# Four fused convolution layers on one core: late jobs forced by their own kind, and an earlier due step for the next chunk's first gates

## The chip, the cores and the metric

The kernel runs on one core of a Trainium2 chip. The metric is the device time of one execution in microseconds (us), the median of several runs. Everything is computed in float32.

## The reference, cut to what matters

The input is x with shape (8, 384, 32, 32): eight images of 384 channels and 1024 positions. Each of four layers adds its result to x, after a group norm over 32 groups.

```python
# layer 0: mamba block (layer 2 is the same with a layer norm ahead and an MLP behind)
xin, z = split(xseq @ in_proj_w.T)              # 384 -> 2 x 768
u   = silu(causal_conv3(xin) + conv_b)
dbc = u @ x_proj_w.T                            # dt (24), B (16), C (16)
dt  = softplus(dt @ dt_proj_w.T + dt_proj_b)
h   = exp(dt * A) * h + dt * u * B              # along 1024 positions, 768 x 16 states
y   = (sum_n h * C + u * D) * silu(z)
x   = x + y @ out_proj_w.T
# layer 1: 1x1 conv, filter on 8x8 patches, 3x3 depthwise conv, gated GELU, 1x1 conv
# layer 2: layer norm, mamba block, then gelu(t @ mlp_w1.T) @ mlp_w2.T
# layer 3: 3x3 depthwise conv
```

## The kernel before

**Chunks and steps.** The two mamba layers set the frame. Each image is cut into two chunks of 512 positions, c = 0 and 1, which gives 16 chunks for layer 0 (n = 0 to 15) and 16 for layer 2 (n = 16 to 31). Each chunk has 24 steps (`NQ`), one for each group of 32 of the 768 inner channels, so there are 768 steps. A step t does the following:

- `times(t + 1)` (L619): two multiplications on POOL (L623) of dt*u by B for the next step.
- `scan(t)` (L637): four scans along 512 positions on DVE (L643), two multiplications by C on DVE (L654) and one of twice the width on POOL (L660).
- `gather(t - 1)` (L664): TensorE sums over the 16 states into y.
- `begin(t + 3)` (L610): a DMA on SP's queue loads dt*u, spread over the states, from the scratch tensor `dud` into a tile g.
- `decay(t + 1)` (L627): TensorE spreads dt into four PSUM banks dA, and ACT takes the exponential.

The four banks dA exist once, so decay(t + 1) waits for the scans of step t.[...]

**Jobs.** All other work is cut into jobs, Python generators whose pieces are put between the parts of a step: `measure` (group statistics of a later image), `front` (L487: load, norm, first projection, convolution, SiLU, dt, B and C of the next chunk), `gates` (L440: z and its SiLU, in two halves of 12 steps each), `finish` (L722: the output projection and, in layer 2, the MLP), `layer1` and `layer3` (once for each image). A job has a first step, a due step ("last") and a kind. The class `Jobs` keeps them: `step` (L133) gives pieces away in order of their due steps, as long as the measured need of such a piece fits the room of the step, counted as TensorE and VectorE time (`ROOM`, L68, and `begin`, L124). The need of a piece is what the same piece took in the last finished job of the same kind (L102). A piece may answer "wait", and the next job in order is asked. `until` (L148) ignores the room: it runs pieces in order of due steps until a condition holds.

**Where work is forced.** At steps 4 and 16 of a chunk `until` asks for the gates of the half in use (L1027). At every step it asks for the `dud` of the step three later (L1041); at steps 21 to 23 that is the next chunk's front. The due steps are given in the main loop, counted from the chunk's first step t: gates of the second half t + 8; the next chunk's front t + 14; the next chunk's first gates t + 26 (`t + NQ + 2`); `measure` t + 28; the end of the chunk before 10, 16 or 23 steps after it; `layer1` and `layer3` of an image near the end of the chunk two later (L732 to L736).

**What jobs wait for.** `front` starts when the second gates of the chunk before are done (L490), and its first projection waits until the chunk two before has finished its output projection ("free", L504, L720). `out_proj` waits for the end of the chunk before and for one of three tiles x (L687), which `layer1` or `layer3` releases when it ends (L858, L991). The first gates wait for the norm and for half of the chunk before (L442). Three PSUM banks are shared by all jobs.

All jobs' matmuls are recorded at one line, L177; all activations at L241; most of the jobs' VectorE work at L85. They are told apart by their tiles: `ps_z` gates, `ps_in`, `ps_x`, `ps_bc`, `ps_dt` front, `ps_out` output projection, `ps_up` and `ps_dn` MLP, `ps_t`, `ps_o` layer 1, `ps_dw` the convolution of layer 1 (with `tp`) or layer 3 (with `xp`).

Of the kernel before, what the change touches and what calls it, by code (L numbers as in the profile page):

```python
# [40 lines left out]
NSUB = 4  # L41
NQ = ND * NSUB
QUADS = [(k, s) for k in range(ND) for s in range(NSUB)]
NH = ND // 2
# [9 lines left out]
def _flat(ap):  # L54
    return ap.rearrange("p a b -> p (a b)")
# [8 lines left out]
WAIT = "wait"  # L64
# [25 lines left out]
class Jobs:  # L90
# [54 lines left out]
                    if went:  # L145
                        break

    def until(self, done):  # L148

        while not done():  # L150
            if not any(self.piece(job) for job in self.in_order()):
                raise RuntimeError("no job goes on")


# [1 line left out]
def tile_conv_preact_d4(ctx: ExitStack, tc: tile.TileContext, a: dict, out: bass.AP):  # L156
# [12 lines left out]
    jobs = Jobs(work)  # L169
# [9 lines left out]
    def ps_tile(name):  # L179

        while live["ps"] >= NBANK:
            yield WAIT
        live["ps"] += 1
        return psg.tile([P, 512], F32, tag="ps", name=name)
# [4 lines left out]
    def pipe(units, deep=2):  # L189


        flying = []
        units = deque(units)
        while units or flying:
            went = bool(flying)
            for f in list(flying):
                if f["stages"]:
                    f["stages"].popleft()(f["ps"])
                settle(f)
                if not f["stages"]:  # L200
                    flying.remove(f)
            if units and live["ps"] < NBANK and len(flying) < deep:
                went = True
                name, stages = units.popleft()
                live["ps"] += 1
                ps = psg.tile([P, 512], F32, tag="ps", name=name)
                stages[0](ps)
                f = {"stages": deque(stages[1:]), "ps": ps, "bank": True}
                settle(f)
                if f["stages"]:  # L210
                    flying.append(f)
            if units or flying:
                yield None if went else WAIT
# [8 lines left out]
    def both(*stages):  # L222


        def run(ps):
            for stage in stages:
                stage(ps)

        return run
# [3 lines left out]
    def act(out_, in_, func, **kw):  # L233

        if func in (AF.Exp, AF.Ln):
            if act_set["now"] != "exp":
                nc.scalar.preload_act_table_set(SET_EXP)
                act_set["now"] = "exp"
        elif func not in (AF.Identity, AF.Copy, AF.Square, AF.Abs):
            act_set["now"] = func  # L240
        nc.scalar.activation(out_, in_, func, **kw)  # L241

    def exp_again():

        nc.scalar.preload_act_table_set(SET_EXP)
        act_set["now"] = "exp"
# [152 lines left out]
    def measure(s):  # L399

        blocks = [(h, k) for h in range(2) for k in range(KC)]
        loaded = {}

        def load(q):
            if q < len(blocks):
                h, k = blocks[q]
                x = loaded[h, k] = wk.tile([P, T], F32, tag="spm", name="xk", bufs=2)
                nc.sync.dma_start(
                    x, s["src"][s["b"], k * P : (k + 1) * P, h * T : (h + 1) * T]
                )  # L410

        live["spm"] = True
        load(0)
        load(1)
        yield NEXT

        def block(h, k):
            return loaded.pop((h, k)), lambda: load(blocks.index((h, k)) + 2)

        def all_read():  # L420
            live["spm"] = False

        s["stats"] = yield from group_stats(block, all_read, NEXT)

    def project(s, d, at):


        def run(ps):
            for k in range(KC):
                mm(  # L430
                    ps,
                    s["w"]["in"][:, k, at + d * P : at + (d + 1) * P],
                    s["xn"][:, k, :],
                    start=k == 0,
                    stop=k == KC - 1,
                )

        return run

    def gates(s, h):  # L440

        while "normed" not in s or (  # L442
            h == 0 and s["n"] > 0 and "half" not in chunks[s["n"] - 1]
        ):
            yield WAIT
        z = s["z", h] = wk.tile([P, NH, T], F32, tag="z", name="z", bufs=2)

        def evict(d):
            return lambda ps: act(z[:, d, :], ps, AF.Copy)

        yield from pipe(
            ("ps_z", [both(project(s, h * NH + d, DI), evict(d))]) for d in range(NH)
        )
        yield EARLY
        act(_flat(z), _flat(z), AF.Silu)
        exp_again()
        s["gates", h] = True
        yield
# [28 lines left out]
    def front(s):  # L487

        c, n = s["c"], s["n"]
        while n > 0 and ("gates", 1) not in chunks[n - 1]:  # L490
            yield WAIT
        xn = s["xn"] = load_half(s)
        if n % (B * NCH) == 0:
# [53 lines left out]
            act(_flat(uh[h]), _flat(uh[h]), AF.Silu)  # L547
        exp_again()
        yield NEXT
        ps = yield from ps_tile("ps_x")  # L550
        for d in range(ND):
            mm(ps[:RX, :], w["x"][:, d, :], u[d], start=d == 0, stop=d == ND - 1)
# [52 lines left out]
        while flying:  # L605
            flying = [f for f in flying if next(f, f) is not f]
            yield NEXT


    def begin(s, i):  # L610
        k, sub = QUADS[i]
        t = s["g", i] = wk.tile([P, 4, T], F32, tag="g", name="g", bufs=AHEAD + 1)
        nc.sync.dma_start(
            _flat(t),
            s["dud"][k][E8 * sub : E8 * (sub + 1)].rearrange("e j t -> e (j t)")
            .unsqueeze(0).to_broadcast([NS, E8, 4 * T]),
        )

    def times(s, i):  # L619

        for j in (0, 2):
            g = s["g", i][:, j : j + 2, :]
            nc.gpsimd.tensor_mul(  # L623
                g, g, s["bc"][:, 0, :].unsqueeze(1).to_broadcast([P, 2, T])
            )
# [11 lines left out]
    def scan(s, i):  # L637

        g = s["g", i]
        own = SHARE[s["pre"]][s["c"]][i % NSUB]  # L640
        for j in range(4):
            q = 4 * i + j
            nc.vector.tensor_tensor_scan(  # L643
                dAs[j] if j < own else g[:, j, :],
                dAs[j],
                g[:, j, :],
                0.0 if s["c"] == 0 else carry[:, q : q + 1],
                ALU.mult,
                ALU.add,
            )  # L650
            if j < own:
                if s["c"] < NCH - 1:
                    nc.vector.tensor_copy(carry[:, q : q + 1], dAs[j][:, T - 1 : T])
                nc.vector.tensor_mul(g[:, j, :], dAs[j], s["bc"][:, 1, :])  # L654
        if s["c"] < NCH - 1:
            nc.vector.tensor_copy(  # L656
                carry[:, 4 * i + own : 4 * i + 4].unsqueeze(2), g[:, own:4, T - 1 : T]
            )
        g = g[:, own:4, :]
        nc.gpsimd.tensor_mul(  # L660
            g, g, s["bc"][:, 1, :].unsqueeze(1).to_broadcast([P, 4 - own, T])
        )
# [307 lines left out]
    def layer3(s):  # L970
# [24 lines left out]
    chunks = [  # L995
        {"pre": pre, "src": src, "b": b, "c": c, "n": (q * B + b) * NCH + c}
        for q, (pre, src) in enumerate((("l0_", a["x"]), ("l2_", x_mid)))
        for b in range(B)
        for c in range(NCH)
    ]  # L1000
# [14 lines left out]
    for t in range(total):  # L1015
        s, i = steps[t]
        n = s["n"]
        later = chunks[n + 1] if n + 1 < len(chunks) else None
        if i == 0:
            jobs.add("gates", gates(s, 1), t + 1, t + 8)  # L1020
            if s["c"] == 0 and n + NCH < len(chunks):
                jobs.add("measure", measure(chunks[n + NCH]), t, t + NQ + 4)
            if later:
                jobs.add("front%d" % (later["pre"] == "l2_"), front(later), t + 3, t + 14)
                jobs.add("gates", gates(later, 0), t + 13, t + NQ + 2)
        if i % (NH * NSUB) == NSUB:
            jobs.until(lambda: ("gates", i // (NH * NSUB)) in s)  # L1027
        if t + 1 < total:
            times(*steps[t + 1])
        scan(s, i)  # L1030
        jobs.begin(ROOM["turn" if n == B * NCH else s["pre"]])
        jobs.step(t, 2.0)
        if t > 0:
            p, q = steps[t - 1]
            gather(p, q)
            if q == NQ - 1:
                end = 10 if p["pre"] == "l0_" else 23 if p["c"] == 0 else 16
                jobs.add("end%d" % (p["pre"] == "l2_"), finish(p), t + 1, t + end)
        if t + AHEAD < total:
            p, q = steps[t + AHEAD]  # L1040
            jobs.until(lambda: p.get("dud", {}).get(QUADS[q][0]))  # L1041
            begin(p, q)
        jobs.step(t)
        if t + 1 < total:
            decay(*steps[t + 1])
# [133 lines left out]
```

## Time and profile before

| | us |
|---|---|
| median of 3 runs | 7789.29 |
| lowest, highest run | 7782.02, 7790.03 |
| the profiled execution | 7774.96 |
| its span, first to last instruction | 7773.2 |
| PE busy in it | 7244.1 |
| DVE busy | 5787.0 |
| POOL busy | 5638.8 |
| ACT busy | 4034.0 |
| mean granted TensorE clock, share of full | 0.922 |

The span is of the profiled execution, which is 14 us faster than the median. A matmul's end in the profile is modelled and matmuls are pipelined, so PE's busy time includes waiting. Busy times are of engines that work beside each other and don't add up. In lines of the timeline the columns are start in us, duration in us, engine, line, operation, tile written and tiles read, shape and count; what stands in square brackets is idle time of the engine before it and what ended it. A float32 matmul counts as two instructions (1152 of them for the 576 matmuls of the output projection).

### The profile page before, as it was taken

The numbers are of one execution on the slowest core, as the hardware profiler recorded it, in microseconds if no ns is written. First come the engines' busy times: TensorE is split into PE (matmuls) and PEld (weight loads), VectorE is DVE, ScalarE is ACT, GpSimd is POOL, SyncE is SP. The second block draws the span as 40 slices with busy tenths as digits, with TensorE's granted clock in tenths as the row PEclk, the third lists the DMA queues.
The fourth block names the chain that finished last, engine by engine and source line by source line (L and its number), as shares of the span: only waits on it lengthen the run. The fifth ranks groups of instructions, "written<-read, shape, count | busy, mean of one in ns | idle before, by whom it ended". The sixth has DMA issues, their size and how long they took to land. (4 is left out here: it accounts for less than half of the span.)

```text
span 7773.2 us, 76689 instructions
## 1 busy us (share of the span) xinstructions
PE 7244.1 (93%) x25762; PEld 3001.0 (39%) x25762; DVE 5787.0 (74%) x7350; ACT 4034.0 (52%) x6980; POOL 5638.8 (73%) x2710
## 2 busy tenths in 40 slices
PE   7989999999999999999999989999999999999998
PEld 2223333333333333333334434444444444444445
DVE  5988788888777878778746765767777677776871
ACT  4445555554554555455545544555555555555543
POOL 5888878788787878778646764767767677676770
PEclk8888889999888999988899999999999999999999
DMA  5666556556565646556536654666656666565662
GB/s 141 141 151 144 138 134 142 136 135 150 127 146 127 141 120 148 128 139 146 129 78 167 174 135 120 165 156 172 165 150 174 155 170 164 149 164 146 171 168 67
DMA packets 288919, 1122.50 MB, mean 144 GB/s; under 512 B 37386, under 2 KB 90970, under 8 KB 190220
## 3 DMA queue, kind: packets, MB, share of 16 engines
q1 hardware_dynamic: 288524, 1117.59, 58.4%
q8 instruction: 204, 3.34, 0.2%
q14 instruction: 191, 1.56, 0.1%
HBM read 1041.96 MB, written 75.50 MB: 144 GB/s over the span
## 5 line engine op out<-in xcount | busy, mean ns | idle before, releaser
L623 POOL TENSOR_TENSOR g<-g,bc 128x1024 f32<-128x1024 f32 x1536 | 3586.8, 2358 | 197.2 <-DMA g<-dud 181.2
L660 POOL TENSOR_TENSOR g<-g,bc 128x1024 f32<-128x1024 f32 x768 | 1806.2, 2352 | 1441.1 <-DVE carry L656 806.6
L241 ACT ACTIVATE dA<-dA,w_A 128x512 f32<-128x512 f32 x3072 | 1860.7, 662 | 1543.3 <-PE dA L177 1530.1
L177 PE MATMUL dA<-dt,selr 32*128 32x512 f32 x6144 | 1573.3, 677 | 70.6 <-DVE g L654 61.9
L643 DVE TENSOR_TENSOR_SCAN dA<-dA,carry,g 128x512 f32<-128x512 f32 x768 | 986.6, 1285 | 616.0 <-issue 275.6
L643 DVE TENSOR_TENSOR_SCAN dA<-dA,g 128x512 f32<-128x512 f32 x768 | 940.6, 1225 | 477.5 <-issue 167.7
L654 DVE TENSOR_TENSOR g<-dA,bc 128x512 f32<-128x512 f32 x1536 | 1053.9, 686 | 29.8 <-DVE dA L643 0.5
L177 PE MATMUL y<-g,sely 128*32 128x512 f32 x6144 | 934.1, 637 | 43.0 <-POOL g L660 37.5
L643 DVE TENSOR_TENSOR_SCAN g<-dA,carry,g 128x512 f32<-128x512 f32 x768 | 940.6, 1267 | 0.0
L643 DVE TENSOR_TENSOR_SCAN g<-dA,g 128x512 f32<-128x512 f32 x768 | 893.3, 1204 | 0.0
L177 PEld LDWEIGHTS dA<-dt,selr 32*128 32x128 f32 x6144 | 470.2, 191 | 984.4 <-DVE g L643 517.3
L177 PE MATMUL ps_dn<-h,mw 128*128 128x256 f32 x2304 | 573.9, 401 | 75.3 <-DMA mw<-in_l_mlp_w 58.6
L177 PE MATMUL ps_up<-t,mw 128*128 128x256 f32 x2304 | 566.8, 394 | 59.0 <-DMA mw<-in_l_mlp_w 44.2
L177 PE MATMUL ps_z<-xf,w_in 128*128 128x512 f32 x1152 | 586.1, 649 | 27.3 <-DVE dt L85 23.6
L177 PE MATMUL ps_in<-xf,w_in 128*128 128x512 f32 x1152 | 566.9, 633 | 27.3 <-DVE u L85 25.5
L177 PE MATMUL ps_dw<-tp,diag 96*96 96x512 f32 x1152 | 572.8, 638 | 15.2 <-ACT diag L241 15.2
L177 PE MATMUL ps_out<-u,w_out 128*128 128x512 f32 x1152 | 543.7, 619 | 10.2 <-DVE x L85 10.2
L177 PEld LDWEIGHTS ps_dn<-h,mw 128*128 128x128 f32 x2304 | 439.5, 197 | 277.0 <-issue 118.8
L177 PEld LDWEIGHTS ps_up<-t,mw 128*128 128x128 f32 x2304 | 425.8, 192 | 268.4 <-issue 148.9
L177 PE MATMUL ps_dw<-xp,diag 128*128 128x512 f32 x864 | 407.5, 622 | 42.2 <-ACT diag L241 40.9
L241 ACT ACTIVATE u<-ps_in,w_vec 128x512 f32<-128x512 f32 x192 | 149.4, 778 | 484.2 <-PE ps_in L177 484.2
L177 PEld LDWEIGHTS y<-g,sely 128*32 128x32 f32 x6144 | 134.2, 111 | 648.5 <-issue 461.1
(99 smaller groups left out, 6463.1 us busy)
## 6 DMA issues: line engine op xcount, KB each, us to landing
g<-dud SPq DMA_DIRECT2D x768, 1024.0 KB, 7.1
mw<-in_l_mlp_w SPq DMA_DIRECT2D x384, 384.0 KB, 7.4
dud<-du SPq DMA_DIRECT2D x768, 64.0 KB, 1.7
xk<-in_x SPq DMA_DIRECT2D x48, 256.0 KB, 4.2
xf<-in_x SPq DMA_DIRECT2D x16, 768.0 KB, 8.4
x<-in_x SPq DMA_DIRECT2D x16, 768.0 KB, 8.5
x_mid<-x SPq DMA_DIRECT2D x16, 768.0 KB, 4.6
xk<-x_mid SPq DMA_DIRECT2D x48, 256.0 KB, 5.0
```

The source lines that it names most:

```text
L177: nc.tensor.matmul(out_, lhsT, rhs, start=start, stop=stop)
L241: nc.scalar.activation(out_, in_, func, **kw)
L623: nc.gpsimd.tensor_mul(g, g, s["bc"][:, 0, :].unsqueeze(1).to_broadcast([P, 2, T]))
L643: nc.vector.tensor_tensor_scan(dAs[j] if j < own else g[:, j, :], dAs[j], g[:, j, :], 0.0 if s["c"] == 0 else carry[:, q : q + 1], ALU.mul ...
L654: nc.vector.tensor_mul(g[:, j, :], dAs[j], s["bc"][:, 1, :])
L660: nc.gpsimd.tensor_mul(g, g, s["bc"][:, 1, :].unsqueeze(1).to_broadcast([P, 4 - own, T]))
```

## The change

The change touches the planner and two waits in `front`; no arithmetic is added or removed.

- `until` takes a kind. Jobs of that kind are asked first, then all jobs in order of due steps.
- The kind "gates" is split into "gates0" and "gates1", so that each half has a history of needs of its own. Forcing at steps 4 and 16 names the half, forcing of `dud` names the front.
- The next chunk's first gates are due at t + 20 (`t + NQ - 4`) instead of t + 26. They now stand ahead of jobs due at t + 21 to t + 25.
- `front` also waits for the image's statistics before it starts, and ahead of `ps_x` for the end of the front of the chunk before ("spread"). Both are waits of the planner: no instruction is added, the piece is placed later.

```diff
-    def until(self, done):
+    def until(self, done, kind=None):
 
         while not done():
-            if not any(self.piece(job) for job in self.in_order()):
+            late = [job for job in self.in_order() if job["kind"] == kind]
+            if not any(self.piece(job) for job in late + self.in_order()):
                 raise RuntimeError("no job goes on")
...
         c, n = s["c"], s["n"]
-        while n > 0 and ("gates", 1) not in chunks[n - 1]:
+        while n > 0 and ("gates", 1) not in chunks[n - 1] or "stats" not in chunks[n - c]:
             yield WAIT
...
         exp_again()
         yield NEXT
+        while n > 0 and "spread" not in chunks[n - 1]:
+            yield WAIT
         ps = yield from ps_tile("ps_x")
...
             flying = [f for f in flying if next(f, f) is not f]
             yield NEXT
+        s["spread"] = True
...
         if i == 0:
-            jobs.add("gates", gates(s, 1), t + 1, t + 8)
+            jobs.add("gates1", gates(s, 1), t + 1, t + 8)
...
-                jobs.add("gates", gates(later, 0), t + 13, t + NQ + 2)
+                jobs.add("gates0", gates(later, 0), t + 13, t + NQ - 4)
         if i % (NH * NSUB) == NSUB:
-            jobs.until(lambda: ("gates", i // (NH * NSUB)) in s)
+            h = i // (NH * NSUB)
+            jobs.until(lambda: ("gates", h) in s, "gates%d" % h)
...
             p, q = steps[t + AHEAD]
-            jobs.until(lambda: p.get("dud", {}).get(QUADS[q][0]))
+            jobs.until(
+                lambda: p.get("dud", {}).get(QUADS[q][0]), "front%d" % (p["pre"] == "l2_")
+            )
             begin(p, q)
```

## The prediction

> **What bounds the kernel now.** I read the page first (shares, slices, the groups of POOL), then the timeline around the two kinds of place where work is forced, then the stretches table for the same places.
>
> ```profile
> span 7773.2 us, 76689 instructions
> ...
> PE 7244.1 (93%) x25762; PEld 3001.0 (39%) x25762; DVE 5787.0 (74%) x7350; ACT 4034.0 (52%) x6980; POOL 5638.8 (73%) x2710
> ...
> PEclk8888889999888999988899999999999999999999
> ...
> L623 POOL TENSOR_TENSOR g<-g,bc 128x1024 f32<-128x1024 f32 x1536 | 3586.8, 2358 | 197.2 <-DMA g<-dud 181.2
> L660 POOL TENSOR_TENSOR g<-g,bc 128x1024 f32<-128x1024 f32 x768 | 1806.2, 2352 | 1441.1 <-DVE carry L656 806.6
> ```
>
> The span has 768 steps, 10.1 us each. POOL needs 2 x 2.358 + 2.352 = 7.07 us in every step; I round to a floor of 7.1. PE's 93% hides waiting, so I take its need from spacing in the timeline:
>
> ```profile
> 3731.86 1.06 PE L177 MATMUL y<-g,sely 128*32 128x512 f32 x8
> 3732.86 1.14 PE L177 MATMUL dA<-dt,selr 32*128 32x512 f32 x8
> 3733.93 2.84 PE L177 MATMUL ps_out<-u,w_out 128*128 128x512 f32 x6
> ...
> 3737.70 15.72 PE L177 MATMUL ps_in<-xf,w_in 128*128 128x512 f32 x36
> ```
>
> The scan's own matmuls take 3733.93 - 3731.86 = 2.07 us a step. Other work goes at about 0.43 us an instruction (15.72/36), and a 128x512 matmul is two of them: 0.86 us. I call that a unit. A step with u units then needs max(7.1, 2.07 + 0.86u); they balance at 5.85 units. The instruction order gives u for every step (between two groups of dA matmuls). A step's time is from the first exponential of one dA group to that of the next. Chunk 23 (5420.6 to 5652.2 us) has 161 units and no large burst: 231.6 us against a need of 24 x 2.07 + 161 x 0.86 = 188.2, so an ordinary step carries 43.4/24 = 1.81 us of waiting between engines. All units sum to 4785.6 in both kernels: the work is the same, so only the waiting and steps below the floor can change the time.
>
> Two places matter. "22.4" is chunk 22, step 4. There the old order forces 36 units (30 of layer 3's convolution and 6 of gates):
>
> ```profile
> 5200.54 10.57 PE L177 MATMUL ps_dw<-xp,diag 128*128 128x512 f32 x24
> ...
> 5212.31 15.72 PE L177 MATMUL ps_dw<-xp,diag 128*128 128x512 f32 x36 [1.20 <-ACT diag L241]
> 5227.86 5.31 PE L177 MATMUL ps_z<-xf,w_in 128*128 128x512 f32 x12
> ...
> 5235.20 2.37 POOL L660 TENSOR_TENSOR g<-g,bc 128x1024 f32<-128x1024 f32 x1 [28.46 <-DVE carry L656]
> ```
>
> POOL idles 28.46 us, but PE waits only 1.20 us. At 16.21 a late front is forced, 31 units:
>
> ```profile
> 3757.08 5.36 PE L177 MATMUL ps_x<-u,w_x 128*57 128x512 f32 x12 [3.66 <-ACT u L241]
> 3763.21 0.69 PE L177 MATMUL ps_bc<-dbc,w_dt 32*128 32x512 f32 x1 [0.77 <-ACT dbc L241]
> 3768.44 1.28 POOL L583 TENSOR_TENSOR du<-dt,u 128x512 f32<-128x512 f32 x1 [13.14 <-DVE dt L85]
> ```
> ```profile
> 3734.00:3769.30 35.30, 30.86 (x86) 11.26 (x86) 17.18 (x25) 17.71 (x23) 10.06 (x10) 0.95 0.23 63
> 3769.30:3774.30 5.00, 3.02 (x11) 0.71 (x4) 4.76 (x8) 2.46 (x6) 5.00 (x3) 0.50 0.22 54
> 3774.30:3788.10 13.80, 13.80 (x37) 4.99 (x38) 12.90 (x22) 5.58 (x9) 9.91 (x6) 0.70 0.70 154
> ```
>
> (Columns: length, then busy PE, PEld, DVE, ACT, POOL; granted clock; DMA share; GB/s.) The front is a chain, and PE waits inside it; the planner then gives step 22 no units at all, and PE's granted clock falls to 0.50 and 0.70.
>
> **What the skill says.** The Trainium skill, "Perfetto Trace Analysis", Identifying the Most-Contended Engine: matmul busy time is no measure of closeness to the peak. It agrees: the need is 4785.6 x 0.86 + 768 x 2.07 = 5705 us, the page shows 7244.1 busy. "TensorE: Matmul & The Clock Gate", Part 1, What's actually happening: the clock is gated by recent activity and halves after an idle window. It agrees: 0.50 in the 5.00 us after the front, 0.97 to 0.99 in full chunks. Same page, Part 2, Step-by-step: matmuls keep program order. It agrees: at 22.4 the y matmuls stand behind all 72 forced instructions, until 5233.10.
>
> **The change part by part.** It adds and removes no matmul.
>
> Forcing by kind at step 4 and 16: the bursts at 20.4 (64.5 units) and at 22.4, 24.4, 26.4, 28.4, 30.4 (36 each) are gone; only gates are forced. Price: steps 4 to 6 of those five chunks take 55.3, 53.6, 53.6, 53.6, 55.3 us for 48 units, a need of 3 x 2.07 + 41.3 = 47.5; 6.8 us of waiting on average, against 3 x 1.81 = 5.4. Gain 1.4 x 5 = 7. At 20.4 to 20.6 it is 87.8 us for 77.5 units, need 72.9: 14.9 of waiting, gain 9. Together -15 (sum of the unrounded terms -16).
>
> The earlier end of the first gates (20 steps instead of 26) and the new order leave the front of the next chunk late. In the new order, step 21 forces a front in every chunk from 19 to 30: 13, 19, 13, 38.5, 16, then 44.5 and 16 in turn. These were ordinary steps of 6 to 8.5 units in chunks 20 to 30, so 11 front bursts are new. Each is followed by a step of 0 or 1 and one of 7 units. Price: steps 21 to 23 of chunk 16 take 54.1 us for 38 units, need 38.9: 15.2 of waiting. The smaller ones in chunks 6, 8, 10 (31.1, 34.9, 42.8 us for 16.5, 18.5, 17 units) give 10.7, 12.8, 22.0, mean 15.2 again. The same three steps without a burst, in chunks 21 to 24 (31.7, 29.4, 31.9, 29.5 us for 21 to 21.5 units), give 7.5, 4.7, 7.7, 4.8, mean 6.2. So 9.0 each, bounds 4.5 and 15.8: 11 x 9.0 = +99. This contains the spills and loads: g<-dud stands on SP's queue behind dud<-du and the MLP weights, POOL waited 1.65 us for it after 16.21.
>
> Steps below the floor: in chunks 19 to 30 outside step 22, the old order has 2 steps of 3 units, the new one 18. A step of 3 units loses 7.1 - 2.07 - 2.58 = 2.45 us of PE that no later step gives back: 16 x 2.45 = +39. Bounds 0 (the neighbour's PE work slides in) and 64 (12.12 and 12.13, 3 and 6 units, took 7.4 + 11.6 us, 4 over two ordinary ones).
>
> Layer 0 and 1: bursts at 8.21 and 10.21 grow from 13 to 25 units. Their waiting goes from 12.8 and 22.0 to the 24.4 of 12.21 (55.6 us for 29 units): +14, bounds 0 and 20. At 16.21 it grows from 31 to 43 with the same chain: 0.
>
> The end: after the last scan 217.5 units stand alone instead of 171, because 46.5 units of layer 3 and the MLP are no longer forced earlier. Those units cost the same 0.86 us at 20.4, uncovered as well, so only waits count: one more wait of down on GELU (3.72 us before ps_dn in the end of the old trace) and the seams of the convolution (1.20 us): +6, bounds 0 and 12.
>
> New waits: "stats" and "spread" are waits of the planner and add no instruction; what they hold back stands in the order and is counted above.
>
> Sum: 99 + 39 + 14 + 6 - 15 = +143 us. The profiled execution is 7774.96 us (span 7773.2): 7918. The median shown, 7789.29, is 14 above it: 7932, which I round to 7930.
>
> **The rivals.** *Faster: slack.* One mechanism, in the ordinary steps of chunks 20 to 30: bursts take units away, 6.7 per step become about 6.45, and PE then absorbs what DVE, ACT and POOL are late. Price: some 11 x 21 = 231 steps, so it decides from 143/231 = 0.62 us a step. For it: 12.1 to 12.20 take 8.34 us for 5.85 units, 1.24 us of waiting. Against: chunk 18 has 6.56 units and 2.18 us of waiting. If waiting falls from 1.81 to 1.0, -0.81 x 231 = -187 + 143 = -44: 7745.
>
> *No change.* The front bursts cost only their low bound and the low steps nothing: 11 x 4.5 - 15 + 0 to 6 = +35 to +41; with slack of 0.15 us a step, about 0: 7789. For it: PE is busy 30.86 of 35.30 us at 16.21. Against: the 4.9 us at 16.22 with hardly any units.
>
> *Slower still: the clock.* PE's holes keep the clock down. Chunk 19, with bursts and low steps, was granted 0.93 and took 256.2 us for 158 units; chunk 23, at 0.99, 231.6 for 161. If all eleven chunks become like it, 11 x 24.6 = +271 in place of 99 + 39: +276, 8065.
>
> That the change doesn't do what it says can be excluded for step 4: the order shows it. That it moves the lateness instead of removing it is my forecast.
>
> **How the numbers follow.** Forecast 0.63, slack 0.15, no change 0.10, clock 0.12. The forecast's own range adds the bounds without all extremes at once: +35 to +250, 7824 to 8040. To leave out no more than two in ten I reach down over most of the no-change case and up to the clock case: 7780 to 8065. About 0.2% (15.6 us) is what a measurement can tell from no change. Faster 0.15, same 0.10, slower 0.75.
>
> **What would show it.** In the new trace: no POOL wait near 28 us at step 4 of chunks 22 to 30; instead at step 21 from chunk 20 on, a wait of POOL on dt of over 13 us, ps_x waiting on u for about 3.7, and a granted clock near 0.5 after it. Pairs of chunks from 24 on should take about 22 us more than the old mean of 489; the stretch after the last scan about 240 instead of 193.4. It is wrong if those pairs stay under 489, or if front bursts carry less than 7 us of waiting.

## The result and the profile after

The changed kernel takes 8056.12 us (median of 4 runs, 8045.03 to 8069.68), the kernel before, beside it on the same chip, 7785.66 us. The ratio is 1.035, with a 95% interval of 1.0331 to 1.0369. The forecast, 7930 us in a range of 7780 to 8065, had the direction; 126 us of the size were missing.

The page of the kernel after, the lines that answer to those of before:

```profile
span 8055.6 us, 76665 instructions
...
PE 7387.0 (92%) x25762; PEld 3054.9 (38%) x25762; DVE 5799.9 (72%) x7350; ACT 4038.2 (50%) x6980; POOL 5637.9 (70%) x2710
...
PEclk8889999899999989898889899998898988998899
...
L627 POOL TENSOR_TENSOR g<-g,bc 128x1024 f32<-128x1024 f32 x1536 | 3585.8, 2356 | 155.3 <-DMA g<-dud 146.6
L664 POOL TENSOR_TENSOR g<-g,bc 128x1024 f32<-128x1024 f32 x768 | 1806.1, 2352 | 1344.1 <-DVE g L647 671.5
```

The instruction counts of PE, DVE, ACT and POOL are those of before, to the last one, and POOL is busy for 1 us less: the work is the same and the span is 282 us longer. From slice 20 on the clock's row alternates between 8 and 9 where before it was a row of nines. (The changed file has four more lines: L178 is the old L177, L664 the old L660.)

Where the lateness went is read from the waits. First POOL's before, then after (columns: total, times, longest):

```profile
POOL g L660 <- DVE carry L656: 806.6, 365, 61.7
...
POOL du L583 <- DVE dt L85: 153.0, 9, 49.2
```
```profile
POOL g L664 <- DVE carry L660: 660.5, 357, 8.6
POOL du L586 <- DVE dt L85: 390.0, 22, 48.9
```

The long waits for the scans, which the bursts at step 4 and at 20.4 made, are gone: the longest fell from 61.7 to 8.6 us. In their place du waits for dt 22 times instead of 9; that is the forced front. The lateness moved, as forecast.

The surprise is in PE's waits. One row before and the same row after:

```profile
PE ps_in L177 <- DVE u L85: 25.5, 29, 3.9
```
```profile
PE ps_in L178 <- DVE u L85: 91.8, 32, 5.3
PE ps_x L178 <- ACT u L242: 71.4, 19, 8.4
```

A projection `ps_in` needs `xf` and a PSUM bank; `u` is what DVE writes from the bank of an earlier projection. A wait of ps_in on DVE u is therefore a wait for a bank. The timeline of the kernel after shows it in one kind of chunk only. First the front forced at step 21 of chunk 24 (columns: start, duration; idle before in brackets):

```profile
5893.65 1.55 PE L178 MATMUL ps_up<-t,mw 128*128 128x256 f32 x6
5895.03 16.00 PE L178 MATMUL ps_in<-xf,w_in 128*128 128x512 f32 x36
5914.70 7.05 PE L178 MATMUL ps_x<-u,w_x 128*57 128x512 f32 x12 [3.67 <-ACT u L242]
...
5928.36 1.27 POOL L586 TENSOR_TENSOR du<-dt,u 128x512 f32<-128x512 f32 x1 [15.45 <-DVE dt L85]
```

and then the one of chunk 25, whose projections begin at step 18:

```profile
6104.85 2.84 PE L178 MATMUL ps_dw<-xp,diag 128*128 128x512 f32 x6
...
6131.01 1.55 PE L178 MATMUL ps_up<-t,mw 128*128 128x256 f32 x6
...
6142.70 4.98 PE L178 MATMUL ps_in<-xf,w_in 128*128 128x512 f32 x6 [5.30 <-DVE u L85]
...
6157.97 5.46 PE L178 MATMUL ps_in<-xf,w_in 128*128 128x512 f32 x6 [3.90 <-DVE u L85]
...
6173.67 4.51 PE L178 MATMUL ps_in<-xf,w_in 128*128 128x512 f32 x6 [3.83 <-DVE u L85]
6181.90 8.38 PE L178 MATMUL ps_x<-u,w_x 128*57 128x512 f32 x12 [3.73 <-ACT u L242]
...
6199.37 1.26 POOL L586 TENSOR_TENSOR du<-dt,u 128x512 f32<-128x512 f32 x1 [24.78 <-DVE dt L85]
```

In chunk 24 six projections of 6 instructions run as one row of 36 in 16.00 us. In chunk 25 a piece comes, PE idles up to 5.30 us for the bank, and after each of the three long holes shown the next piece takes 4.5 to 5.5 us instead of 2.84, because most of it runs at half the clock (granted 0.50 from 6140.23 to 6147.05 us, for the first). The two lines ahead say who has the other banks: at 6104.85 layer 3 began a group of nine taps and got only three done, at 6131.01 the MLP began an up unit. Neither goes on before the front's projections are done: the next `ps_up` piece runs at 6212.38, the next `ps_dw` piece at 6240.81. The group of taps stays open for 143 us, from step 15 of chunk 25 to step 2 of chunk 26. In the kernel before, the groups of chunks 21 to 29 that stay open for long (38 to 40 us) begin at step 20, behind the front's projections. Two of the three banks are held by half-done work, and the front has one, which ACT and DVE must empty each time.

The stretches of the two groups (columns as in the prediction: length, busy PE, PEld, DVE, ACT, POOL, granted clock, DMA share, GB/s):

```profile
5879.60:5929.30 49.70, 45.26 (x112) 17.50 (x116) 15.98 (x22) 21.40 (x30) 7.53 (x9) 0.92 0.17 56
5929.30:5934.20 4.90, 3.69 (x11) 0.68 (x4) 4.73 (x8) 2.36 (x6) 4.90 (x3) 0.50 0.22 55
6133.60:6164.90 31.30, 20.53 (x60) 6.91 (x56) 18.68 (x21) 12.22 (x20) 19.13 (x9) 0.78 0.31 71
6164.90:6203.30 38.40, 24.82 (x52) 7.18 (x56) 10.67 (x13) 15.00 (x22) 6.28 (x4) 0.76 0.03 7
```

Chunk 24's front (49.70 us, 44.5 units) has PE busy for 91% of it. Chunk 25's takes 31.30 + 38.40 us for 12 + 16 units, at a clock of 0.77. As whole chunks: the odd chunks 23 to 29 went from 231 to 235 us each to 275 to 279, the even ones 24 to 28 from 249 to 261 to 271.

### The profile page after: what moved, and what is told of

Same layout as the page of the kernel before. It is cut to its first block, busy times and chain, and to the rows that moved or that the text cites. A ratio compares the mean times of both kernels' runs of the same rounds, so it can differ in the third digit from the quotient of the medians.

```text
span 8055.6 us, 76665 instructions
## 1 busy us (share of the span) xinstructions
PE 7387.0 (92%) x25762; PEld 3054.9 (38%) x25762; DVE 5799.9 (72%) x7350; ACT 4038.2 (50%) x6980; POOL 5637.9 (70%) x2710
## 5 line engine op out<-in xcount | busy, mean ns | idle before, releaser
L664 POOL TENSOR_TENSOR g<-g,bc 128x1024 f32<-128x1024 f32 x768 | 1806.1, 2352 | 1344.1 <-DVE g L647 671.5
L178 PE MATMUL dA<-dt,selr 32*128 32x512 f32 x6144 | 1628.9, 689 | 75.4 <-DVE g L658 66.3
L178 PE MATMUL y<-g,sely 128*32 128x512 f32 x6144 | 965.7, 646 | 53.7 <-POOL g L664 50.3
L178 PEld LDWEIGHTS dA<-dt,selr 32*128 32x128 f32 x6144 | 490.2, 195 | 1018.5 <-DVE g L647 499.7
L178 PE MATMUL ps_in<-xf,w_in 128*128 128x512 f32 x1152 | 577.0, 646 | 93.5 <-DVE u L85 91.8
L178 PE MATMUL ps_dn<-h,mw 128*128 128x256 f32 x2304 | 573.3, 403 | 76.5 <-DMA mw<-in_l_mlp_w 51.4
L178 PE MATMUL ps_up<-t,mw 128*128 128x256 f32 x2304 | 592.3, 407 | 42.3 <-ACT h L242 20.8
L178 PE MATMUL ps_out<-u,w_out 128*128 128x512 f32 x1152 | 563.0, 637 | 23.4 <-DVE x L85 23.4
L178 PE MATMUL ps_dw<-tp,diag 96*96 96x512 f32 x1152 | 565.7, 631 | 16.1 <-ACT diag L242 16.1
L178 PE MATMUL ps_z<-xf,w_in 128*128 128x512 f32 x1152 | 566.2, 629 | 3.2 <-DVE tpix L85 1.7
L178 PEld LDWEIGHTS ps_up<-t,mw 128*128 128x128 f32 x2304 | 444.9, 200 | 272.7 <-issue 162.9
L178 PEld LDWEIGHTS ps_dn<-h,mw 128*128 128x128 f32 x2304 | 444.1, 199 | 268.2 <-issue 107.8
L586 POOL TENSOR_TENSOR du<-dt,u 128x512 f32<-128x512 f32 x192 | 244.1, 1272 | 392.6 <-DVE dt L85 390.0
L178 PE MATMUL ps_dw<-xp,diag 128*128 128x512 f32 x864 | 428.2, 640 | 55.7 <-ACT diag L242 53.0
L85 DVE SCALAR_TENSOR_TENSOR u<-ps_in,w_vec,u 128x511 f32<-128x511 f32 (+1 forms) x384 | 283.8, 746 | 255.1 <-ACT xt L242 130.6
```

The lines of the kernel that those rows point to most:

```text
L85: return call(out_, *args, **kw)
L178: nc.tensor.matmul(out_, lhsT, rhs, start=start, stop=stop)
L586: nc.gpsimd.tensor_mul(v, s["dt"][d], u[d])
L664: nc.gpsimd.tensor_mul(g, g, s["bc"][:, 1, :].unsqueeze(1).to_broadcast([P, 4 - own, T]))
```

## The experiments

A chunk's time runs from its first exponential to that of the next chunk; "waiting" is, as in the prediction, what is left of it after 2.07 us a step and 0.86 us a unit. Where the order of instructions is named, it is that of TensorE's program. Ratios are against the kernel before on the same chip.

**Each half of the change alone.** One kernel keeps the forcing by kind and the two waits, with the old due step; the other has the new due step and the two waits, and forces as before.

```diff
 kind_only:
-                jobs.add("gates0", gates(later, 0), t + 13, t + NQ - 4)
+                jobs.add("gates0", gates(later, 0), t + 13, t + NQ + 2)
 due_only:
-            late = [job for job in self.in_order() if job["kind"] == kind]
+            late = []
```

> The changed kernel with the first gates due at t + 26 again, so that only the forcing by kind (with the split kinds and the two planner waits) is left of the change. The instruction order shows the same front bursts at step 21 of chunks 20 to 30 (44.5 and 13 units in turn) and none at step 4; layer 0 is as before the change. Theory 1 (the order of forcing lets layer 3 fall behind, and the front pays): 8000 to 8060, that is nearly all of the 270 us. Rival (the earlier due step does the harm): below 7830.

> The changed kernel with forcing in order of due steps as before; the earlier due step of the first gates is what is left. The order shows front bursts at step 21 of chunks 20 to 30 again (38.5 and 16 units), here because the gates are no longer late at step 4 and so force nothing else. Theory 1 (either part alone takes layer 3's forcing at step 4 away): 8000 to 8070. Rival (only the forcing by kind does harm): below 7830.

Measured: 8089.88 us (1.0404, 1.0373 to 1.0435) and 8069.8 us (1.038, 1.0344 to 1.0415). Each half gives the whole loss; the first a little more than expected. Either one takes away the forcing at step 4 that used to push layer 3 through, and that is enough for the backlog. ps_in waits for DVE u for 80.3 and 91.8 us in them. The two kernels share the split kinds and the two waits of `front`, which could be the cause instead. No run has these alone, but the program rules them out: with only these added, the kernel before keeps its order of instructions on every engine, except that two pieces of gates in chunk 0, of three matmuls each, come one place earlier.

**The held bank taken away.** The changed kernel, where layer 3 may not begin a group of taps in the second half of an odd chunk (a group in progress may go on). No computation is left out.

```diff
+                if job["kind"] == "layer3" and not job.get("banks") and t % 48 >= 36:
+                    continue
```

(`banks` counts the PSUM banks that a job holds between its pieces.)

> The changed kernel, in which layer 3 may not begin a group of nine taps in steps 12 to 23 of an odd chunk, so that no half-done group holds one of the three PSUM banks while that chunk's front runs. Theory 2 (a half-done convolution group and a half-done MLP unit hold two banks, the front has one and waits for each bank's release): chunks 25, 27, 29 fall from 275 to about 245 us, PE's waits ps_in on DVE u fall from 91.8 us to below 45, and the whole is 7900 to 7960. Rival (the low granted clock after PE's holes sets those chunks): they stay over 265, the whole over 8020.

Measured: 7915.22 us (1.0172, 1.0142 to 1.0201). Of 270 us, 141 are gone, although fronts are still forced at step 21, with up to 50 units. In its PE waits the row of ps_in is back to its old size:

```profile
PE ps_in L182 <- DVE u L85: 22.8, 18, 3.9
```
```profile
6083.30:6101.60 18.30, 17.47 (x66) 6.89 (x63) 17.95 (x21) 8.15 (x16) 13.98 (x6) 1.00 0.50 112
6101.60:6119.90 18.30, 17.13 (x54) 7.24 (x52) 9.52 (x11) 14.01 (x19) 10.22 (x5) 0.88 0.26 68
```

The second fence is from the stretches table of the same kernel: its steps 25.19 and 25.20 (66 matmul instructions, 60 in the changed kernel) and its step 25.21. They take 18.30 + 18.30 us where the changed kernel took 31.30 + 38.40, and the clock is 1.00 and 0.88. The clock rose when the holes went, with nothing done to the clock. Chunks 25, 27, 29 take 239.7, 248.1, 236.1 us. In steps 18 to 23 of the odd chunks 21 to 29 the waiting falls from 215 to 98 us, which is most of the 141.

**The same bank taken on purpose.** Two kernels in which a 32x32 matmul writes a PSUM tile and a copy of one column reads it some steps later, which keeps a bank from the jobs. All other instructions, of TensorE and of the other engines, keep their order, so little but the bank differs.

```diff
+    def hold(until):
+        ps = yield from ps_tile("ps_hold")
+        mm(ps[:32, :32], sely[:, 0, :], sely[:, 0, :])
+        while now[0] < until:
+            yield WAIT
+        vector.tensor_copy(kept, ps[:32, :1])
+        ps_done()
...
 after_hold, in the changed kernel:
+        if n in (22, 24, 26, 28, 30) and i == 16:
+            jobs.add("hold", hold(t + 6), t, t - 24)
 before_hold, in the kernel before:
+        if n in (21, 23, 25, 27, 29) and i == 11:
+            jobs.add("hold", hold(t + 11), t, t - 24)
```

> The changed kernel with one PSUM bank occupied on purpose (a 32x32 matmul writes it at step 16 of chunks 22, 24, 26, 28, 30, a copy reads it at step 22); the order of all other TensorE instructions is the same. Bank theory (the odd chunks' front groups are dear because a half-done depthwise group holds one of the three banks): the even chunks, which had two banks free, lose what the odd ones lose, 14 to 27 us each: 56 to 135 in all, 8110 to 8190, and the waits of ps_in on DVE u grow from 91.8 us to over 150. Rival (odd groups are dear for another reason, such as the MLP's work beside them): no change, 8040 to 8080.

Measured: 8209.82 us (1.0535, 1.0505 to 1.0565), 154 us above the changed kernel, somewhat more than expected. The even chunks 22 to 30 go from 263, 271, 271, 271, 281 to 299, 303, 303, 303, 314 us, the odd ones stay at 274. The same front of chunk 24 in its timeline, and its row of waits:

```profile
5931.80 2.74 PE L178 MATMUL ps_in<-xf,w_in 128*128 128x512 f32 x6
5937.06 4.51 PE L178 MATMUL ps_in<-xf,w_in 128*128 128x512 f32 x6 [2.53 <-DVE u L85]
5944.10 4.51 PE L178 MATMUL ps_in<-xf,w_in 128*128 128x512 f32 x6 [2.53 <-DVE u L85]
```
```profile
PE ps_in L178 <- DVE u L85: 155.6, 57, 5.3
```

A projection comes every 7.04 us (5944.10 - 5937.06) instead of every 2.67 (16.00/6). The same chain of work is dearer when one bank is missing.

> The kernel before with one PSUM bank occupied in the same way from step 11 to 22 of chunks 21, 23, 25, 27, 29; the order is otherwise that of before, with no burst at step 21. Bank theory: the front and the MLP share two banks, of which a half-done up unit holds one from step 13 on; 8 to 25 us more in each of the five chunks, 40 to 125 in all: 7825 to 7910. If a missing bank costs only when the front is forced in a burst: within 15 us of before, 7770 to 7800.

Measured: 8026.69 us (1.031, 1.0288 to 1.0332), 242 us above before and far over the expectation: 43 to 52 us in each of the five chunks (239, 232, 231, 234, 235 us become 282, 280, 283, 280, 278). In these chunks nothing of the front is forced: a missing bank costs without any burst. The timelines of step 25.16, before and with the bank held:

```profile
6049.72 1.02 PE L177 MATMUL ps_dt<-dbc,w_dt 25*128 25x512 f32 x2
6050.67 2.86 PE L177 MATMUL ps_dn<-h,mw 128*128 128x256 f32 x12
6053.45 1.06 PE L177 MATMUL y<-g,sely 128*32 128x512 f32 x8
6054.45 2.86 PE L177 MATMUL ps_dn<-h,mw 128*128 128x256 f32 x12
```
```profile
6196.23 1.02 PE L177 MATMUL ps_dt<-dbc,w_dt 25*128 25x512 f32 x2
6197.18 1.56 PE L177 MATMUL ps_dn<-h,mw 128*128 128x256 f32 x6
6204.18 2.93 PE L177 MATMUL ps_dn<-h,mw 128*128 128x256 f32 x6 [5.44 <-DVE dt L85]
6207.04 1.93 PE L177 MATMUL y<-g,sely 128*32 128x512 f32 x8
6208.90 3.56 PE L177 MATMUL ps_dn<-h,mw 128*128 128x256 f32 x12
```

The MLP's second group of `ps_dn` finds no bank until DVE has read ps_dt (5.44 us), and DVE reads it only after the four scans that stand ahead of it on its queue. y stands behind ps_dn, and what follows runs at half speed (y 1.93 for 1.06). The stretches of the three steps 25.16 to 25.18 with that bank held, and the same three before:

```profile
6196.40:6247.70 51.30, 35.12 (x127) 19.54 (x127) 23.07 (x26) 13.35 (x24) 25.20 (x13) 0.80 0.44 114
```
```profile
6049.90:6079.10 29.20, 26.21 (x128) 15.44 (x127) 22.89 (x26) 13.36 (x23) 25.57 (x13) 1.00 0.69 175
```

That splits the price: of 22.1 us more, 13.2 are more idle time of PE (51.30 - 35.12 = 16.2 against 3.0), and 8.9 are more busy time for the same matmuls, at a clock of 0.80 instead of 1.00.

**A forced front by itself.** The kernel before, where the fronts of chunks 23, 25, 27, 29, 31 may not start ahead of step 20 of the chunk that prepares them.

```diff
+        while n in (23, 25, 27, 29, 31) and now[0] < NQ * n - 4:
+            yield WAIT
```

> The kernel before, where the fronts prepared in chunks 22, 24, 26, 28 and 30 may not start ahead of step 20, so that step 21 forces 37 units of front there, with no layer 3 group held; by its order the rest stays near the kernel before (two of its five bursts at step 4 go, two grow to 48 units, 13 units are forced at step 21 of two odd chunks, the end gets 12 units more). The price of a front burst with two banks free, as the even chunks of the changed kernel show it, is 12.5 us above the same three steps of before: 5 x 12.5 and 10 to 15 for the odd ones and the end: 7850 to 7875. If forced fronts cost nothing of themselves and the held bank is all: 7770 to 7805.

Measured: 7975.29 us (1.0253, 1.0221 to 1.0285), 100 us above the expectation. Forced fronts do cost of themselves: steps 21 to 23 of the five even chunks carry 131.0 us of waiting instead of 25.8, 21.0 more each. That exceeds the 12.5 us of the changed kernel. These groups contain the layer norm too, which the changed kernel has done earlier; the timeline of 24.21:

```profile
5925.88 4.54 PE L177 MATMUL ps_lv<-sq,ln_mean 128*128 128x512 f32 x6 [1.92 <-ACT sq L241]
5933.32 17.64 PE L177 MATMUL ps_in<-xf,w_in 128*128 128x512 f32 x36 [2.90 <-ACT xf L241]
5954.62 8.18 PE L177 MATMUL ps_x<-u,w_x 128*57 128x512 f32 x12 [3.66 <-ACT u L241]
```

A longer forced chain lays more waits bare: 1.92, 2.90 and 3.66 us here, and the pieces after them run slowly (4.54 us for 6 instructions, 8.18 for 12). The profiled execution is 218 us longer than that of before, and 105 of them lie in these steps. In the steps 0 to 20 of the odd chunks 21 to 29 the waiting grows by 46 us, in their steps 21 to 23 by 30 (12 units are now forced in chunks 23 and 27), and in chunk 31 ahead of the end by 28. There dt steps and gates had to follow the late fronts; these parts weren't separated further.

**More room for the planner.** Room of layer 2 raised from 6.4 to 7.0, in the changed kernel, in the kernel before, and in the changed kernel with layer 3 kept from beginning a group anywhere in odd chunks (`t % 48 >= 24` in the edit above).

```diff
-ROOM = {"l0_": (5.2, 3.0), "turn": (6.4, 3.0), "l2_": (6.4, 3.0)}
+ROOM = {"l0_": (5.2, 3.0), "turn": (7.0, 3.0), "l2_": (7.0, 3.0)}
```

> The changed kernel with a room of 7.0 instead of 6.4 us of TensorE work a step in layer 2. In the order no front is forced at step 21 from chunk 21 on and nothing large at step 4. Theory 1 (the loss is a backlog: the room gives fewer units than the 7.2 a step that layer 2 has, so something must be forced, and the change only chose what): 7650 to 7760, faster than both kernels. Rival (the bursts are cheap and steps over 7 units cost as much as they bring): 7950 to 8060.

> The kernel before with the planner's room of layer 2 raised from 6.4 to 7.0 and nothing else. By its order the forced layer 3 at step 4 of chunks 22 to 30 is gone, step 21 forces no front there, and layer 3 is done by step 12 of the odd chunks, so that no half-done group stands beside the front. Theory (time is lost in bursts and with a bank missing): 7690 to 7765, faster than before. Rival (an even load just above the floor costs as much waiting as bursts do, as the 240 to 242 us of the even chunks with this room would say): 7770 to 7850.

> The changed kernel with room 7.0 and layer 3 not allowed to begin a depthwise group in odd chunks. The timeline of the run with room 7.0 alone shows the half-done group from step 11 to 19 of its odd chunks (270 to 282 us each); without it they should take about 240: 5 x 30 = 150 less, some 20 to 40 of it given back at step 21 of the even chunks (13 units forced) and at the end (207 units instead of 153). Bank theory: 7740 to 7800 (from 7889). Rival (the odd chunks are slow because of their 179 units): 7860 to 7910.

Measured: 7889.0 (1.0139, 1.0109 to 1.0169), 7857.81 (1.0093, 1.0071 to 1.0115) and 7905.21 us (1.0153, 1.013 to 1.0177). All three miss on the slow side. In the first, the forced fronts of chunks 22 to 30 are gone and its even chunks take 239 to 242 us, but a half-done group of layer 3 now stays open from step 11 or 12 to 20 or 21 of the odd chunks from 23 on (in chunk 21 from 16 to 22), and the odd chunks stay at 270 to 282. Without it (third run) the odd chunks 21 to 29 fall from 1370 to 1284 us in sum, but the even chunks from 22 on give back 36 us, chunk 20 another 13, and chunk 31 with the end 54, where 207 units stand alone instead of 153. So the held bank is seen there too, yet room 7.0 isn't a way to a faster kernel: in the kernel before it costs 0.9% though its order forces nothing from chunk 20 on. Many of its steps alternate between 9 units and 6 or fewer, and in its chunk 21 a group of layer 3 is open from step 12 to 19; whether either is the cause wasn't tried.

**The earlier due step in layer 0 alone.** The kernel before with one edit; from chunk 16 on its order is that of before.

```diff
-                jobs.add("gates", gates(later, 0), t + 13, t + NQ + 2)
+                jobs.add("gates", gates(later, 0), t + 13, t + NQ - 4 if n < 15 else t + NQ + 2)
```

> The kernel before with one part of the change in layer 0 only: the next chunk's first gates are due at step 20 instead of 26 up to chunk 14; from chunk 16 on the order is that of before. The forecast's own term for layers 0 and 1 says 14 us slower (0 to 20): 7790 to 7810. The traces say otherwise: chunks 3 to 15 took 2827 to 2844 us in the five runs with the earlier due and 2854 to 2871 in four without it, 30 us less: 7745 to 7770, faster than both kernels by a little.

Measured: 7759.49 us (22 runs, against 7785.76 in 27 of before), ratio 0.9972, 0.996 to 0.9983: faster than both kernels, by a quarter of a per cent. The gain is small beside what one profile can show: chunks 3 to 15 take 2847 us in its profile and 2854 in that of before, while chunks 16 to 19, with the same order, differ by 20 us the other way. It stands on the medians.

## Why the prediction was right, and where its size failed

Waiting, in us, from the two profiles (the units are the same in sum, so this adds up to the whole 282):

| where | before | after | more | forecast |
|---|---|---|---|---|
| steps 21 to 23, chunks 20 to 30 | 70.5 | 258.6 | +188 | +99 |
| of these: even 22 to 30 | 25.8 | 88.5 | +63 (12.5 each) | 9.0 each |
| of these: odd 21 to 29 | 40.0 | 143.6 | +104 (20.7 each) | 9.0 each |
| steps 0 to 20 of odd 21 to 29 | 189.6 | 271.2 | +82 | part of +39 |
| steps 0 to 20 of even 22 to 30 | 200.1 | 215.3 | +15 | part of +39, and -7 |
| steps 0 to 20 of chunk 20 | 66.2 | 33.0 | -33 | -9 |
| chunks 16 to 19 | 293.3 | 329.4 | +36 | 0 |
| chunks 0 to 15 | 1117.8 | 1105.4 | -12 | +14 |
| chunk 31 and the end | 80.5 | 87.8 | +7 | +6 |

The 22 us of the first row that the next two leave are those of chunk 20. Rows of 20 us or less are within what two profiles of the same order can differ by.

*Direction and main place: right.* The bursts at step 4 went and front bursts at step 21 came, with their marks: du waiting 15.45 and 24.78 us on dt, ps_x 3.67 and 3.73 on u, a clock of 0.50 in the 4.90 us after. Taken in pairs (24 with 25, and so on to 29), two chunks took 489 us before and 546 after in the mean, +57 where about 22 was forecast.

*The range: in part luck.* The measured time lies above the forecast's own bounds, which end at 8040 us. It lies within the stated range only because that was stretched up to the clock rival's 8065.

*The step that failed: "9.0 each" for all eleven front bursts.* It was one price for every burst, taken from chunks 6, 8, 10 and 16. For the even chunks it was somewhat low (12.5). For the odd ones it was far too low: 20.7 in the group itself, and another 40 us over five chunks in steps 18 to 20, where the small bursts had begun early. A price that grows with the burst (16 units against 44.5) would have said the reverse. What decides between odd and even here is how many PSUM banks the front finds: with the bank free, steps 21 to 23 of the odd chunks cost 8.0 us each above before, close to the 9.0. The description of the kernel had the fact (three PSUM banks for all jobs), but the sum never asked who holds them. The Trainium skill says it plainly ("Perfetto Trace Analysis", Matmuls): independent groups should rotate through different banks so that the emptying of one overlaps the next group's matmuls. This case agrees and gives the price: 2.67 us for a projection with two banks free, 7.04 with one.

This is shown from both sides: taking the half-done group away brings 141 of the 270 us back, and taking a bank away, with every other instruction in place, makes a like loss in the even chunks and in the kernel before. With the bank free, the changed kernel stands at 7915 us, close to the forecast's 7932. The forced fronts are a large part of that, but the other terms don't match one by one, so the agreement of the sums is partly chance. Even with two banks free the price isn't one number: with the layer norm in the chain it was 21.0 in the kernel with late fronts.

*Steps below the floor, +39: not settled, and not nothing.* The changed kernel has 15 steps of 3 units in chunks 20 to 30 outside steps 21 to 23. They take 95.4 us for 45 units, 1.7 us of waiting each, which is the ordinary 1.8; 9 of them last 4.8 to 5.6 us, below POOL's 7.1. But the steps just after them wait for 6.3 us each, 95 in all and 68 above the ordinary. Steps 25.12 to 25.15, of 3, 6, 3 and 6 units, in the stretches table:

```profile
6065.80:6072.92 7.12, 7.08 (x32) 3.15 (x30) 7.05 (x13) 6.62 (x9) 6.56 (x3) 1.00 1.02 323
6072.92:6089.06 16.14, 15.67 (x49) 6.31 (x49) 10.19 (x11) 5.86 (x10) 10.31 (x9) 0.79 0.57 166
6089.06:6093.90 4.84, 4.84 (x17) 1.51 (x17) 4.02 (x5) 4.70 (x9) 4.36 (x2) 1.00 0.64 135
6093.90:6108.78 14.88, 13.51 (x35) 4.25 (x35) 12.21 (x14) 6.70 (x12) 11.49 (x5) 0.77 0.46 115
```

No wait for a bank stands in these four steps. In steps 0 to 17 of the odd chunks 21 to 29 the waiting is 158 us before, 199 after and still 188 with the bank free, so the held bank explains little of that. Whether the low steps cause it, or the work that fell into the steps after them (group statistics, the layer norm), no run tells.

*Layers 0 and 1, +14: wrong in sign.* The kernel with only that part is 26 us faster (13 to 31 by its interval).

*Chunks 16 to 19, +36, counted as nothing:* chunk 19 went from 256.2 to 275.3 us and falls to 223.0 when layer 3 may not hold the bank (with 11 units fewer, while chunk 20, which does more then, grows by 26); it is an odd chunk of the same kind, one earlier than the sum began. The other 16 us are within the scatter of one profile.

*The end:* 193.4 became 229.8 us for 217.5 units, where about 240 was forecast; its waiting was even 4 us less.

*The rivals.* Slack and no change are refuted by the interval. The clock rival's number, 8065, lies nearest to the result, and half of its mechanism holds: holes in PE do lower the clock, and 8.9 of the 22.1 us in the three steps shown of the kernel before with a held bank are slower matmuls. But the holes in steps 18 to 21 of the odd chunks are waits for a bank, not a property of low steps; filled, the clock of steps 25.19 and 25.20 returned from 0.78 to 1.00. In steps 25.13 and 25.15, granted 0.79 and 0.77, the rival may be right: a low step stands ahead of each.

Not settled: what the steps after low steps wait for, why room 7.0 makes the kernel before slower, the part of the late fronts' cost that lies after them, and where in layer 0 the 26 us are won.

## What to carry to other kernels

When work is cut into pieces and reordered, list what each piece holds between its parts, PSUM banks above all; a half-done accumulation that is overtaken can cost every later group its overlap. A price per burst is valid only for the same number of free banks and the same chain: look in the timeline for a matmul group waiting on the reader of an earlier group of its own kind. And forcing work that seems too early may be what keeps a chain on time: look at what will be late once it is no longer forced.

## What the hardware showed that was not expected

A short hole in PE can be paid twice. This is the front of chunk 24 with the bank held, in the changed kernel, cut where the granted clock changes (columns as above):

```profile
5937.83:5941.24 3.41, 3.41 (x5) 1.01 (x3) 0.00 (x0) 0.00 (x0) 0.00 (x0) 0.50 0.00 0
5941.24:5944.65 3.41, 0.88 (x3) 0.34 (x3) 1.50 (x2) 0.78 (x1) 0.00 (x0) 1.00 0.00 0
5944.65:5948.07 3.42, 3.42 (x6) 1.24 (x4) 0.00 (x0) 0.00 (x0) 0.00 (x0) 0.50 0.00 0
5948.07:5951.48 3.41, 0.88 (x3) 0.30 (x2) 1.50 (x2) 0.78 (x1) 0.20 (x1) 1.00 0.00 0
```

The clock alternates, and out of step with the work: PE is busy through the whole of each half-speed stretch and for 0.88 of 3.41 us of each full-speed one. So the full speed falls on the holes of 2.53 us and the half speed on the matmuls, and each of the five later projections takes 4.47 to 4.51 us instead of 2.84. The Trainium skill, "TensorE: Matmul & The Clock Gate", Part 1, What's actually happening, says that the clock halves after an idle window. Here the stretch ahead of each halving was not idle throughout: the 0.88 us of work in it did not prevent the halving. At 16.21 of the kernel before, from which the prediction took that the skill agrees, PE counts as busy for 2.64 of the 3.41 us ahead of the halving at 3765.54. Not every hole costs this. In chunk 25 of the changed kernel, six instructions took 2.81 us after holes of 1.52 and 1.17 us, and in the kernel before the twelve of ps_x at 16.21 took 5.36 us after one of 3.66, at full speed.

Executions of the same order differ by more in one part than one might think: chunks 0 to 15 took 3463, 3478, 3482 and 3488 us in the profiles of the kernel before and of its three variants with a held bank, with room 7.0 and with late fronts, whose edits touch later chunks only. Differences of 20 us over many chunks can't be read from one profile.
